# Four graph layers on one core: turned tiles read back from DRAM by one DMA, a new order of the work, dummy products on TensorE

## The chip, the cores and the metric

The kernel runs on one core of a Trainium2 chip. The metric is the device time of one execution in microseconds (us), the median of several runs. A core has TensorE (PE in the profile: matmuls; PEld: the loads of its weights), VectorE (DVE), ScalarE (ACT), GpSimd (POOL) and SyncE (SP). Here SP does nothing but issue DMAs, in order, on one queue.

## The reference, cut to what matters

64 graphs of 256 nodes with 256 features, and a 256 x 256 adjacency matrix each, go through four layers. Each one is `x = x + layer(relu(layernorm(x)), adj)`, all in float32:

```python
# layer 0: eight heads of 32
scores = where(adj > 0, q @ k.T / sqrt(32), -1e9);  x += (softmax(scores) @ v) @ Wo + bo
# layer 1: one head, softmax over axis 1
e = leaky(f1[:, None] + f2[None, :]);  x += elu(softmax(where(adj > 0, e, -9e15), axis=1) @ Wh)
# layer 2: three rounds of messages and a GRU cell
m = h @ weight[i];  aggr = A.T @ m;  h = gru(aggr, h)
# layer 3: four heads of 64
logits = leaky(s_src[:, None] + s_dst[None, :]);  out = softmax(where(adj == 1, logits, NEG)) @ f
```

Attention weights leave the softmax with a query in each partition, and the product that follows wants a key in each partition. So a 128 x 128 turn stands between them; one is needed too behind each norm and between the rounds of layer 2.

## The kernel before

**Tiles.** Two graphs make a pair, so there are 32 pairs. A pair's `x` is one tile of 128 partitions x 1024 (four chunks of 128 tokens). Most other tiles (`w4`, 21 slots) have this size too, 512 KB. The eight banks of PSUM (`ps`) hold 128 x 512 each.

**Tasks and order.** The functions `layer0` to `layer3` (L805, L940, L1054, L1225) do not issue instructions. They hand tasks to `Plan.add` (L195): an engine, a cost in us, a function that issues the instructions, and the buffers read and written. Some tasks have two forms, for instance an eviction on ACT or on DVE (`evict`, L414) or an addition on POOL or DVE (`either`, L421). `ORDER` (L48) is a compressed table, searched offline: it gives each of the 13,630 tasks a rank and a form. `Plan.order` (L240) walks the tasks by rank, gives each buffer the slot that comes free first by its estimated times, and returns the list in which every engine's instructions are issued. So each engine runs its own share of this list, in order, and waits where data is late. A DMA is taken to last its issue cost plus 1.4 times its `latency` (`SLOW`, L46 and L269). About six pairs are in flight at once.

**Turning through DRAM.** `through_dram` (L720) is used by `turn` (L732, attention weights), `turn_chunks` (L749, between rounds of layer 2) and `turn_rows` (L764, behind a norm). VectorE first turns blocks of 32 x 32 within the tile (STREAM_TRANSPOSE at L734, L755, L768). One DMA writes the 512 KB tile to a DRAM tile (L723). Four DMAs of 128 KB read it back (L726), each into 32 partitions, so that block column b of each block row lands in partitions 32b to 32b+31. The small turn at the end of layer 3 has the same shape (L1316, L1320, L1323). Tiles read back this way are `mixed`: their columns are in block order, and their readers use strided views (`wide`, `turned_keys`, `by_block`).

**Who turns how.** `TURNED` (L578) names the norms of layers 0 and 2 and the rounds of layer 2; they go through DRAM in all pairs but the last. The norm of layer 3 is turned by TensorE: eight 128 x 128 transposes against the identity (L664), then an eviction with relu on ACT (L676) or DVE (L677). The attention weights of layers 0 and 3 go through DRAM (those of layer 3 in the last pair by TensorE, L744).

**Products.** Most PE time goes to the gates of layer 2 (L1124, 128 x 512). The scores of layer 0 use 32-row tiles of the array (mode "rows", L844), its context product 32-column tiles ("columns", L896), layer 3's product 64-column tiles ("halves", L1300).

**Layer 3's end.** Per graph, eight `scalar_tensor_tensor` on DVE (L1334) scale the read-back tile by the reciprocal sums and add it to `x`. In layer 0, POOL adds the bias `bo` to `x` (L811).

Of the kernel before, what the change touches and what calls it, by code (L numbers as in the profile page):

```python
# [19 lines left out]
P = 128  # L20
# [17 lines left out]
class Task:  # L38
    __slots__ = ("pair", "forms", "form", "bufs", "rank", "stage", "mode", "before", "end", "engine", "latency")


class Plan:
# [3 lines left out]
    SLOW, SWITCH = 1.4, 0.19  # L46

    ORDER = (  # L48
        "c-rlI2Y_T%m3Ezb?|b*<S2=f8=iJki6U>kqh9FVNf`bxFxW-*vcSZDHRM1_+qO7>AxQa?rRz*hQNQMbaf?;y%?&;}R)m{1B{}wPamAa>TNTS"
        "m)-PKk1y?fvJ&iT%F&b^JSGxS-RKJ<7U64EsK?}%Y0r__{_Uj7&8U+e;ezYbn~=5t^|8eRr>NB1*mH>9AK9{<I<U8uk53z1K3{?Urxi6f5Qp"  # L50
        "L85YtP5wZZ@SSCI;`VY0Agr<EfaDCgryJGK(Ao(E2C;o?=fQTkzr5V#aIKFa#Nd>s5>pHWbHM_>$|64w^(2_*j$qy`J@LNQq%PQK<`58FlP~"
        "$<JEDo{#ESp7_z7CW5ce#tL#Wpf@eThz7NR=y5@}0kspJe)|$O2>umFYylNhQC@e^E0f2Te%2str2(qFGNjvbbF{ERFq&#gcA0UPGtUekhbK"
        "zCz59hn_{m1x->~fk2lAxkK5COxG4=@6cgSv;5{*V21VINSEKmd^d+9c365cS8qMSiO%HR#X)9F3MmcZz7~N&rF#&^iobfD~eh`*egbjDW`9"
        "1wS{JiI^V?IT=JRjmdV)g^7hzpaA%lfSSNr6;c5exo0VTkD-*FLK(XqA;2x$VwXE4A>5x~^YO*0(Ns-Z8EHf?cZ}|Ro=W?iIjO%@f|j(N{lF"
        "^(Ajq;fOlUfYEj(+LOfBDnTFVj;Q&WGwgD4zb1BRd<TA*t~%`kGt2w)}I5IoJfU%t^TWxRn?#&#&*@MA(e$GCUezY|mvYHL7g>}m7T`VRq?#"
        "a<*~S1$!06|SaI?rJwi9ylkKX#1j1Nx0A@quIKznsS=L2V;Z&PAbFBXrLcJR&!}8hnz5uH%%izMqC^snY$s33X}lK3a9*;8%pV-Ifm4%U)_x"
        "!v(Fa)2us26bgfXND^Q&Nztg2Q0e*rn0&ExS>iPJmXFqv@0JYL4h{#cZeLy;qL^qH+&|oLB3o4(bHBDH6%#>CNU<?50oe=H?IHP%m{&@H_nZ"
        "U!II>@i49iv=xMzdVQQZPr%aX5Pe47jt9<K967n%TJDNE!Q04f)RNPi=lS*54@PpFx3^R4Cro4H!p<EG+`(kG?#Y#x`{+E@56gMjq1B2~Um>"
        "bqF<vnA2P!fE}x;HW0G22i)-3=_a^+bB?is>pKB%xbhS3JwgIokd=nuCI}6&&Ax2&dP5A1tLC}#hTzXcZCs_7tZCo=q^JUd=C(oC*T6n%8ke"
        "l>02SQmwaBj8y?YmI-Oo-${sA|cZ=hX2c7ss^i;+lfk^n^dkter)^oGs=fUqDf<R~)X?u#Y<38>t42()L!R9}>PAmd&|I8F%S5_f)-5l?-Dh"  # L60
        "zNyzG?6ue0|v;yvR{sGjh+DCUMk!Vu48L<gtn@n+2LLn%tQQ^-F`@1V4n%!mTJ&GEW6w)9)wf84MWY}hpwOlKU&`+=Hsd!$aq9~?Z*EmxNbW"
        "}4d8}Lc|f{Gr(f(`bdn@K8TNoL!f_gv$7g0_)-?i@A(G?PgII8f7!&FR<g#Zn2q`h7=op{d_{({ZZ%ub)(S|M+XrrXs*PX2+9Evlc1!_qgt1"
        "N4^fN*JYqxHw^+)ZQF>`gNP!a^=|`JZ(Jp`?-XA*O{X6Ysf{hbzpiM=U3@lODV5W2FAmzpmdASmznV=R^DE+SjmuuP@c4r)22Zeeu5Ub@~~?"
        "?XF?#y4iM4Blxnrq?Kv|GjWuXTq78Zmjg1#<4AR+hE#BgxJxi!c^SkERc5(gN+v+gh{B?{!5+mTr`nlW&UUy3?)->Zt14E*2sas;m&@c{nGF"
        "OIA_N3M=XUHRVaW4dbf*-h*xMkE+XF)5tU4i}eGDFeD?NS}UA;6ie#sLj-;SckImx#jALdsG!5O1z9yhu^EZ8Bgc)0mtx@5dG?~&On35~Yk?"
        "F!gM9<z(aSaPM`VK=2S>;4@+<k2B8WcR3$)L*hIH6ZQ<hbVYKoW(5Gy3c3vEP*g;+SJn8W8Vv=nD;WMBR)=q(rCi2DG=^R2tOZ`u`d=U5e%K"
        "_nCY6W0BIaaqb~4dlR*}F%^L;U6q}a)y=IN@pi3we8Z0LG>?T01z{DVb=4*B~j9&c!20@v9u>~*AW6BewH@h|1cg}N;J@f9C{!AFkQgxiD*$"
        "^PR{VU%;^LM{i!4CSluby__bCSfAK=2afJ8N-=;DgpgYhb?P!|-k0%3ShCn6qoY7u*g^kBPLqujZsW4Njo_^!j$Bbi!%7S>jhZY6DmRbnq-~"
        "8T193rCIK@nMo)Rs<m>kW;PXIh(EpLnpcC!zt^2;7X|ysyls-;6rqmN;Zt`lLa$yhyY6!GlVfZ2u;Jb2cYai<7jBZzGeEi@iRTfpli52xo+p"
        "&{<^jcNALBWy4%O_G!Q<XC>)EK_sz>()XwU^B@<(>bj`qDy?qQ1_gz15(DN+ow5ex5daGpS0y<i{+qiMOUP@`I+W1JIRy|Le;$3qtBaSR4H5"  # L70
        "%`l4Z73(Z`rLLAo$P(4?lwK`=;QymOM632FArVCoiCDNauCgucT&#$Oc(7WOpFyTHLhB+t_wJ~Mx>benLqMGTNjfhALPho{a)*qFN;XT^JY2"
        "6G)_8S|M(aLT<gE{(KDZG=w10WX~tUS5HmIXCa&3iDqMTN$8&4gx6enX^)_w0&t=5AP~)`q{u|VjWq@P$Ipqd|^?<<XkT&JU2fE-C9((J)Is"
        "AcUfO-ha%f`MK@c?|G@r==~$37|%oxtM8z%xJew!o~FZk`3zXm1D`F7T$6)m;LRv;>^1DVGJq;PnFO2}Sq04DPsw2->2ayUu-L*>d!0_&$6_"
        "KQlUa%MuWzo~4(cDMl2$&W~XM5?~IkA6gfldEz<&RFO)i7=g{r;PCf_*MZ%s;WhGff$&UQM`66F$qGG)&VomvGw4C}gbM|n)z%9TBJgZ&hzk"
        "?Dy*`OEjXn!wjVHc(f#HUv+=C<`?hr9}Swz$lNfRec19{UOj++A`qBF?>7xDZ-(bL9_4FO7%HK=p%%pod?BW@5H<8|=AZQ~S4!_*|uW@U}Jd"
        "l7~1G|EL#LTR<UDR-Q5N`g}?;JoLvesYcTl?8EbXn>VVVumyz%1B_rT~0^btDL;=WB>bK4qx1^EnD`$$+hNUJGf{6=ubn_p>3XN`Xt%>#_=~"
        "ogO1&ajE?0&o|Hs6{NE3D-uY`UH&X4Vnjd#v6Lt)@`>wg?L_CvpTE=lT$Bnx^;)9@Ag2iPA8t{W8hvgJ`_E?a(eDm`JZRh63+`lmQtrMOR^@"
        "JB@NIUHx+VYfd`KQ;ymy|iahgJF5Q`Ver@~4L11Py3GyLnCyK$|j68PjrbZ2MD9E=YhM1s$MZUEsm6O|@$vY*8EYet_%5Om?oYmrrvh{U7@h"
        "Wa^a5K)>A6^o*f}05-_bpnwkD3F4^Z+H~3`36M~?ql1``6b#r!IF2qWLib~hrV|aIv<y*rk~<p8<`it`UX*Zbx|)mD5KdWL(2-Mi1S~UY1ff"
        "M6VXN>^otOp7!8Ik2+*h99YBHS6Xda}a?=lZt@(2ZD_jmNj4p&x)|M{Axe#0LgG6ZRtWEu&3`_}wrLLNBv>%aK<@-OFQyz`Em(sRB8$OX0Xb"  # L80
        "@O&!Ot~T5|Mb!)@BK#WqYyE&-7iK#^QMLcZOo0nbl>^#DV3(@cs}w6?X$<}M$8KxYLfhCTcEE?s#~%m^V!g6?1~B|A~H#GNa`F&X3x#wD^2P"
        "E>017*`b$a&f5bFxe+AhSP8!{L#ohmsyAykS+dS98ciYb9(Rz*?)i_&`pPdE@5_fX-(F{~vl3L?-pFJXbLW0tVgg`A%b|A<gkpb+-3VL3F#a"
        "yXCV_L~6up62T>EiDxXL*q-D-yU#PJc}yDu&%Sn3v_GBc{n7k<r?I?g%D|cSVK(k(ixp3e3fUgDE6q5y3%t5N4!}){dZL2?-~HIx7U3d0bjH"
        "i76I^W{~<C2BiH>3ho?qXI8F{XofUMgNp8jl(zB=lV`M;f=nqx&&N(h5JcSpFwMPN2r%ixFJNVTU;`KN{l|`?1Y)yRaV?6lKsh>aT+6IqJ_#"
        "O%(SxzMXKV&JX_)8CdU);QrXDw;Id|a;D=zvRp3dD2h$hqyr;s!2Mvb1n@Ew%6Q1F=eDT#lqb7rU~p!$;EQd?hb^LFlR%bZpJQ+d>sM2VMHy"
        "gUF;3ri`FawSd21njU>iM#!_0QYWTT#F8ZD2k{y*#}E}PtVys{Ts7?3QwU1v=~15=n|7719!B#3>O+k5ah{?G@=vT4>?cpG2}vVZg;ndN4)N"
        "&D_OIiKrO&u8uh4(5%MII6#o?~_-x-T-t&l^>lr_hw9&vCMevHAN8G%kk`**Pi?xP~!AlC6uc%>2Z`k7=P-E`6EFjsB%^VPH5mj=)Y3t?8qg"
        "Ko%#k7p>hp2`9&s_%;HSu_Ag2qwBa@co^e9oE9baEw&#cJ7*)rwKn(nm&);qtDIi(jsV2q?tBR!}xUj0AhafX=w;gYM?7O)(I}O}hX16`GLd"
        "`a}drpUSC08gKsO!uh7iFw9vB|MQqs!`;xUWwL$w7$e8Ow(L{g>M!gaLU@1Np+mE^&!A}y2d+!}{tujkkZ|RS<DcAPkX#6K+`4Y9%;h+l&xV"
        "aNr~d$gF*gE7!eC64ozaXXuQ-;IdXjPp)R0d|J0+ejxb`{!ehG=l=Z*z-o|9RA`uf&w@J09`T#svRMtf_tI{uiSJ;|V9=ohgR;WA{7BfHn-o"  # L90
        "bDrta$Yf@2G{gc+Qd0<A2&0G7fhJN!PNqm6Vmp?9iM1yhDYI2MHb|g8;`XPcwX`wZa~l5L%IY8Ze$K6Xklf>dhCcdio1dyo+dCQ7B`0O$@-O"
        ")n2}OS0Bdz=L;r1h%qfl9ld>Y#&sgo+a221bCIvziHSmm<Fb8$FM4H|Gp%?L}WvKgne1+}tG|jbvB5Q&UKCYC1DtevZkxU*cjp`_BB52u_$N"
        "L6bb_9ULBe{$2rCFTe=@PUgw-Jzs9@z2ih8oO}BL1oGGb^!~k>v=QvFtcX7=;DH%hb<D??ugAjc1smYJs&bJxgK5Eu&YSraA=-S8jC$ZZnOf"
# [189 lines left out]
def tile_adj_preln_d4(  # L283
# [100 lines left out]
    def buf(tag):  # L384
        return Buf(tag, tiles[tag])
# [1031 lines left out]
```

## Time and profile before

| what | before |
|---|---|
| median of 3 runs (lowest to highest) | 3498.58 us (3495.51 to 3502.81) |
| the profiled execution: its time, its span | 3501.53 us, 3499.7 us |
| mean granted TensorE clock | 0.993 |
| PE, DVE, ACT, POOL busy in 800 to 1600 us | 99.6%, 91.3%, 73.6%, 14.3% |
| DMA engines, mean busy share | 69.3% |
| DMAs: turn writes, read-backs | 535 and 2140 of the large, 62 and 248 of the small |

"Busy" of PE is the time covered by its records, each as long as its pipeline, so short gaps do not show in it; the distance from one start to the next does show them. A line such as "PE ps L664 <- DVE w L625: 5.8, 2, 3.5" says that TensorE's instructions of line 664, writing a `ps` tile, waited for VectorE's of line 625, writing a `w` tile: 5.8 us in 2 waits, the longest 3.5. In a timeline the columns are start, length, engine, line, operation, tiles, and how many instructions were merged.

### The profile page before, as it was taken

Reading aid. Unit: us, or ns where it says so; the run is one execution under the profiler, and the core shown is the slowest. Engines: PE = TensorE matmul, PEld = TensorE weight load, DVE = VectorE, ACT = ScalarE, POOL = GpSimd, SP = SyncE. Lnnn points to the kernel's source line nnn. Section 1 sums busy time; section 2 is a strip of 40 time slices with the busy share of each in tenths; the row PEclk is TensorE's granted clock in tenths of the full one; section 3 lists DMA queues with packets and bytes.
Section 4 is the critical chain, followed back from the end, with each engine's and each line's share of the span. In section 5 each row is a group of like instructions: output and inputs, shape, how many; then the busy total and the mean of one; then the engine's idle time right before and its main releaser. Section 6 shows DMA issues by size and latency. Waiting matters only on the chain.

```text
span 3499.7 us, 53732 instructions
## 1 busy us (share of the span) xinstructions
PE 3433.5 (98%) x14784; PEld 1931.6 (55%) x14784; DVE 3078.1 (88%) x9047; ACT 2522.0 (72%) x6739; POOL 453.1 (13%) x497
## 2 busy tenths in 40 slices
PE   8899999999999999999999999999999999999997
PEld 5555555555555555555555555555555555555554
DVE  8788998999999989999899888999889989889767
ACT  7756786766776777777767777778777768668545
POOL 1010110111111111111111111111011111011010
PEclk9999999999999999999999999999999999999998
DMA  8655877777677777777776777777677776576444
GB/s 287 209 150 167 248 240 217 224 229 228 212 217 233 226 222 235 223 225 225 218 230 215 228 227 216 235 230 234 214 228 216 234 224 218 183 220 201 155 131 136
DMA packets 596081, 753.41 MB, mean 215 GB/s; under 512 B 99012, under 2 KB 507076, under 8 KB 595780
## 3 DMA queue, kind: packets, MB, share of 16 engines
q1 hardware_dynamic: 595780, 749.98, 69.3%
q8 instruction: 118, 1.93, 0.2%
q14 instruction: 183, 1.50, 0.1%
HBM read 426.78 MB, written 314.59 MB: 212 GB/s over the span
## 4 chain that ended last, share of the span: by engine, by line
PE 64%; DVE 7%; DMA 3%; ACT 2%; issue 1%; SPq 1%; POOL 0%; DVEq 0%; ACTq 0%; POOLq 0%
PE ps L1124 37%; PE ps L823 4%; PE ps L1101 4%; PE ps L1246 3%; PE ps L844 3%; PE ps L1300 2%; PE ps L699 2%; PE ps L1031 2%; PE ps L896 2%; PE ps L1017 2%; PE ps L911 2%; DMA w<-turn 2%; DVE w L792 1%; DVE w L954 1%; DVE x L1334 1%
## 5 line engine op out<-in xcount | busy, mean ns | idle before, releaser
L1124 PE MATMUL ps<-w,whhT 128*128 128x512 f32 x2304 | 1071.2, 594 | 1.2 <-DVE mx L792 1.0
L1124 PE MATMUL ps<-w,giT 128*128 128x512 f32 x2304 | 1064.9, 593 | 0.0
L799 ACT ACTIVATE w<-w,mx 128x256 f32<-128x256 f32 x1536 | 759.2, 499 | 45.2 <-DVE mx L792 43.7
L1124 PEld LDWEIGHTS ps<-w,giT 128*128 128x128 f32 x2304 | 435.9, 190 | 534.5 <-issue 511.2
L1124 PEld LDWEIGHTS ps<-w,whhT 128*128 128x128 f32 x2304 | 430.4, 190 | 496.3 <-issue 451.4
L734 DVE STREAM_TRANSPOSE w<-w 128x1024 f32<-128x1024 f32 x380 | 466.4, 1234 | 45.2 <-ACT w L876 25.7
L417 ACT COPY w<-ps 128x512 f32<-128x512 f32 x431 | 244.2, 579 | 198.1 <-PE ps L1300 79.0
L792 DVE CUSTOM_DVE_ANT_0 w<-ps,mask 128x256 f32<-128x256 f32 x1024 | 370.8, 417 | 14.7 <-PE ps L844 12.6
L876 ACT ACTIVATE w<-w,rz 128x256 f32<-128x256 f32 x678 | 292.4, 498 | 88.4 <-DVE rz L869 85.1
L619 ACT ACTIVATE w<-x,rs 128x256 f32<-128x256 f32 x464 | 244.7, 591 | 93.3 <-DVE rs L611 88.9
L799 ACT ACTIVATION_READ_ACCUMULATOR w<-w,mx 128x1 f32 x1536 | 293.4, 191 | 0.0
L1181 POOL TENSOR_TENSOR w<-w,w 128x512 f32<-128x512 f32 x86 | 114.0, 1332 | 1147.9 <-PE ps L1124 368.4
L1277 ACT ACTIVATE w<-w,f 128x256 f32<-128x256 f32 x512 | 219.5, 499 | 16.1 <-DMA w<-row 10.0
L1101 PE MATMUL ps<-part,part 128*128 128x256 f32 x1536 | 228.8, 299 | 1.8 <-DVE part L1091 1.7
L605 POOL TENSOR_SCALAR rs<-mv 128x4 f32<-128x4 f32 x129 | 40.9, 317 | 1368.0 <-DVE mv L594 1301.1
L1149 ACT ACTIVATE w<-ps,brz 128x512 f32<-128x512 f32 x192 | 129.3, 677 | 123.1 <-PE ps L1124 113.4
L1101 PEld LDWEIGHTS ps<-part,part 128*128 128x128 f32 x1536 | 197.3, 190 | 32.1 <-issue 18.3
L792 DVE CUSTOM_DVE_ANT_0 w<-w,mask 128x256 f32<-128x256 f32 x512 | 196.4, 428 | 13.3 <-ACT w L1277 12.4
L1176 ACT ACTIVATE w<-w,bih_sb 128x512 f32<-128x512 f32 x192 | 136.5, 716 | 97.4 <-DVE w L1172 97.3
L592 DVE BATCH_NORM_STATS2 st<-x 128x6 f32<-128x256 f32 x512 | 189.1, 411 | 10.8 <-DMA x<-in_x_dram 8.2
L1163 ACT ACTIVATE w<-ps,brz 128x512 f32<-128x512 f32 x192 | 129.2, 677 | 75.5 <-PE ps L1124 73.1
L1154 DVE SCALAR_TENSOR_TENSOR w<-w,w 128x512 f32<-128x512 f32 x192 | 132.6, 692 | 44.4 <-ACT w L1149 28.1
(117 smaller groups left out, 5132.7 us busy)
## 6 DMA issues: line engine op xcount, KB each, us to landing
turn<-w SPq DMA_DIRECT2D x535, 512.0 KB
w<-turn SPq DMA_DIRECT2D x2140, 128.0 KB
w<-in_adj_dram SPq DMA_DIRECT2D x128, 512.0 KB
w<-row SPq DMA_DIRECT2D x64, 512.0 KB
x<-in_x_dram SPq DMA_DIRECT2D x64, 256.0 KB
out_dram<-x SPq DMA_DIRECT2D x64, 256.0 KB
turn<-w SPq DMA_DIRECT2D x62, 256.0 KB
w<-turn SPq DMA_DIRECT2D x248, 64.0 KB
```

The source lines that it names most:

```text
L417: (A, act(n), lambda: nc.scalar.copy(dst(), src())),
L592: nc.vector.bn_stats(st()[:, t, :], tok(xt())[:, t, :])
L619: nc.scalar.activation(tok(xn())[:, t, :], tok(xt())[:, t, :], func, bias=rs()[:, 1, t : t + 1], scale=rs()[:, 0, t : t + 1])
L734: add((V, dve(T * N), lambda: nc.vector.transpose(blocks(), blocks())), writes=[e])
L792: nc.vector.tensor_tensor_reduce(row, src, mask, scale, 3.0e38, ALU.add, ALU.min, mn)
L799: nc.scalar.activation(row(e, r), row(e, r), AF.Exp, bias=mn()[:, r : r + 1], scale=-1.0, accum_out=zs()[:, z0(r) : z0(r) + 1])
L823: mm(ps(), w[:, k, o * P : (o + 1) * P], wide(hT, k), start=k == 0, stop=k == 1)
L876: op(row, row, rz()[:, r : r + 1])
L1101: mm(ps()[:, o * N : (o + 1) * N], chunk_of(part(), h.mixed, c, o), tok(ams[g](), N)[:, c, :], start=i == 0 and c == 0, stop=i == 1 and c ...
L1124: mm(ps(), w[:, k, c0 : c0 + P], wide(src, k), start=n == 0, stop=n == 2 * len(terms) - 1)
L1176: (A, act(N2, 1), lambda o=o, hn=hn: nc.scalar.activation(at_o(hn, o), at_o(hn, o), AF.Tanh, bias=bih_sb[:, 4 + o : 5 + o])),
L1277: nc.scalar.activation(dst, src, AF.Prelu, bias=f()[:, t, D + h : D + h + 1], alpha=ALPHA)
```

## The change

1. **One read-back.** The four reads become one DMA over all 128 partitions: partition p = 4j + b takes block column b of row j. So that the result comes out in the order wanted, VectorE's block transposes read their source with a distance of four elements between neighbours (L768, L755 and L1316), and so do the mask (L784), the keys in TensorE's scores product (L847) and ScalarE's first step in layer 3 (L1276).
2. **Layer 3's norm** goes through DRAM as well, in all pairs but the last.
3. **Layer 3's product** is cut into 32-column tiles; its end is two multiplications by the reciprocals and one addition, on POOL or DVE. Adding `bo` may go to DVE too.
4. **The plan** models DMAs anew: per DMA an issue time, a time `dma` on one shared lane, a `latency` and 1.2 us of `LANDING`, with eight in flight at most, in place of 1.4 times a latency. The order is searched anew (11,870 tasks). Many costs are refitted.
5. **Dummy products.** Where the plan expects PE to idle for over 1 us (after its first 20 us) and a PSUM bank is free, it inserts 128 x 128 transposes of the identity worth half of that idle time.

```diff
-    TURNED = ("0", "2", "2m",)
+    TURNED = ("0", "2", "3", "2m")
...
+            if engine == "SP":
+                begin = max(begin, lanes[0])
+            if engine == "PE":
+                idle = begin - free.get("PE", 0.0)
+                spare = [slot for at, slot in slots["ps"] if at <= free.get("PE", 0.0)]
+                if idle > self.IDLE and spare and begin > 20.0:
+                    out.append(lambda n=int(self.FILL * idle / 0.11), slot=spare[0]: self.busy(slot, n))
+                    now = "full"
...
-            t.end, t.engine = begin + us + t.latency * self.SLOW, engine
+            if engine == "SP":
+                free["DMA"] = max(free["SP"], free.get("DMA", 0.0)) + t.dma
+                t.end, t.engine = free["DMA"] + t.latency + self.LANDING, engine
+                lanes = lanes[1:] + [t.end + 0.1]
...
+    def busy(slot, n):
+        for i in range(n):
+            nc.tensor.transpose(tiles["ps"][slot][:, 0:P], ident, ident)
...
     def through_dram(e, eT):
         d = buf("turn")
-        add((SP, 0.6, lambda: nc.sync.dma_start(d(), e())), reads=[e], writes=[d], latency=4.6)
-        for b in range(4):
-            add(
-                (SP, 0.55, lambda b=b: nc.sync.dma_start(
-                    eT()[32 * b : 32 * b + 32, :].rearrange("p (a w) -> p a w", a=4),
-                    d()[:, b * N : (b + 1) * N].rearrange("(a j) w -> j a w", a=4))),
-                reads=[d], writes=[(eT, b)], latency=3.8,
-            )
+        add((SP, 0.41, lambda: nc.sync.dma_start(d(), e())), reads=[e], writes=[d], latency=1.41, dma=1.36)
+        add(
+            (SP, 0.5, lambda: nc.sync.dma_start(
+                eT().rearrange("p (a w) -> p a w", a=4),
+                bass.AP(tensor=d().tensor, offset=d().offset, ap=[[N, P], [32 * T * N, 4], [1, N]]))),
+            reads=[d], writes=[eT], latency=2.04, dma=1.9,
+        )
...
-                e().rearrange("p (b x i) -> p x b i", b=4, i=32), xn().rearrange("p (x b j) -> p x b j", b=4, j=32))),
+                e().rearrange("p (b x i) -> p b x i", b=4, i=32), xn().rearrange("p (x j b) -> p b x j", b=4, j=32))),
...
-                                tok(kT(), N2)[r, cc, g * N : (g + 1) * N].rearrange("p (c b j) -> p b c j", c=2, b=4),
+                                else tok(kT(), N2)[r, cc, g * N : (g + 1) * N].rearrange("p (c j b) -> p b c j", c=2, b=4),
...
+                            for r in range(0, C3, 32):
+                                mm(
+                                    pso()[j * C3 + r : j * C3 + r + 32, k * N : (k + 1) * N],
+                                    f()[:, 2 * g + c, h * C3 + r : h * C3 + r + 32],
...
+                def divided(o=o, rz=rz):
+                    for j in range(2):
+                        oj = o().rearrange("p (j a y i) -> p j a y i", j=2, a=2, i=32)[:, j]
+                        rj = rz().rearrange("p (y j) -> p j y", j=2)[:, j]
+                        nc.vector.tensor_tensor(oj, oj, rj.unsqueeze(1).unsqueeze(3).to_broadcast([P, 2, 4, 32]), ALU.mult)
...
+                add(either(0.0, to_x), reads=[o], writes=[(xt, g)])
```

The table's bytes can be read without running anything: the last third of them is each task's form. Counted over pairs 3 to 28, per pair: VectorE takes 2.0 of the 4 scalings behind the norms of layers 0 and 3 (0.58 before), 2.5 of the 6 casts L1085/L1086 (0.62), 1.04 of the 2 new additions to `x`, 0.5 of the 2 additions of `bo` (none); the shares of the other tasks shift by less. Changes between full products and tiled ones number 10.5 a pair (10.0 before).

## The prediction

> **What bounds the kernel.** I read the page's first lines, then the chain, the timeline of one pair, TensorE's waits, and the group rows of what the change touches.
>
> ```profile
> span 3499.7 us, 53732 instructions
> PE 3433.5 (98%) x14784; PEld 1931.6 (55%) x14784; DVE 3078.1 (88%) x9047; ACT 2522.0 (72%) x6739; POOL 453.1 (13%) x497
> ...
> PE 64%; DVE 7%; DMA 3%; ACT 2%; issue 1%; SPq 1%; POOL 0%; DVEq 0%; ACTq 0%; POOLq 0%
> ```
>
> PE is busy 98% of the span and carries the chain. VectorE follows at 88%; in the middle (800 to 1600 us) it stands at 730.5 of 800 us, 91%. In the chain, the same step comes back once a pair:
>
> ```profile
> 2365.94 7.06 PE ps L823 x16
> ...
> 2470.89 7.06 PE ps L823 x16
> ```
>
> That is 104.95 us a pair. In a timeline of PE around there, instructions follow without a gap, the transposes of layer 3's norm among them:
>
> ```profile
> 2438.63 1.88 PE L1124 MATMUL ps<-w,giT 128*128 128x512 f32 x4
> 2440.35 1.04 PE L664 MATMUL ps<-ident,w 128*128 128x128 f32 x8
> 2441.22 1.88 PE L1124 MATMUL ps<-w,whhT 128*128 128x512 f32 x4
> ```
>
> From start to start the eight transposes take 0.87 us, 109 ns each. So I counted PE's time by starts: each kind of instruction at its usual distance to the next (429 ns for 512 columns, 216 for 256, 109 for a transpose, a quarter of 216 on a 32-wide tile) makes 3328 us. A change between full and tiled products adds 93 ns (523 in place of 429); 10.0 of them a pair are 30 us. The first product starts at 6.9 us, the last ends 4.8 before the end. What remains, 3499.7 - 3328 - 30 - 11.7 = 130 us, is waiting and slow clock: about 39 in the first 200 us, 63 in the middle, 28 after 3440. TensorE's waits on read-backs (the columns are us in total, times, longest), and two rows of the chain that show a turn's DMAs when they are waited for:
>
> ```profile
> PE ps L896 <- DMA w<-turn: 12.8, 4, 8.4
> ...
> PE ps L1300 <- DMA w<-turn: 2.0, 1, 2.0
> ```
>
> ```profile
> 2981.34 5.66 DMA w<-turn
> ...
> 3185.46 6.47 DMA turn<-w
> ```
>
> **Layer 3's norm leaves TensorE.** 31 pairs lose eight transposes: 31 x 0.87 = 27.0 us. PE runs without gaps there, so this stands on the path; what is late next is the next product, ready already. In exchange a pair gets one more STREAM_TRANSPOSE, one more 512 KB write and read, and a relu from SBUF in place of one from PSUM. The new wait is relu on DMA: behind it stand the four products of L1246 and, on ACT or DVE, whatever the order put there. A pair is in flight for some 620 us and six overlap, so some ten microseconds more latency is covered by other pairs' products; without that cover it costs a pair 5.66 + 6.47 = 12 us once, at the end, where pair 30 may show it.
>
> **Mode changes.** 10.5 rather than 10.0 a pair: 0.44 x 0.093 x 32 = +1.3 us. Cutting layer 3's product into 32 columns is free by the rows: two products take 3.59 us at L896 (32 columns) and 3.60 at L1300 (64).
>
> **VectorE.** The rows of what it gains and loses:
>
> ```profile
> L768 DVE STREAM_TRANSPOSE w<-w 128x1024 f32<-128x1024 f32 x62 | 76.7, 1238 | 17.3 <-ACT w L619 11.6 <-PE ps L1124 5.2
> ...
> L1334 DVE SCALAR_TENSOR_TENSOR x<-w,rz,x 128x64 f32<-128x64 f32 x496 | 111.9, 296 | 0.2
> ```
>
> Per pair: transpose +1.24; scalings +1.42 x 2 x 0.457 (L625) = +1.30; casts +1.88 x 0.415 (L1086) = +0.78; additions to x 1.04 x 0.69 (L1218) = +0.72; four multiplications of 128 x 256, by L1221's and L876's rows about 0.37 each, +1.5; sixteen of L1334 at 111.9/496 = 0.226, -3.6; other forms cancel. Sum +1.9 us. Today 0.913 x 104.95 = 95.8, then 97.8 of a pair's 104.1 us: 94%. It stays below PE, and costs nothing while it does.
>
> **Distance-four reads.** No row has them. Touched per pair: three transposes of L768 (3.7 us), three of L755's pairs (3.9), two of L1316 (1.4), four halves of the mask L782 (1.8), in all 10.8 us of VectorE; on PE four score products (4.3 us). From below 0: L734 in place, L768 and L755 with scattered runs all take 1.2 to 1.3 ns an element, so the order of reading has bought nothing so far. From above I take a doubling: 10.8 us of DVE and 4 x 0.85 of PE a pair. The nearest row is L755, whose blocks already lie scattered over the tile in runs of 32: 688 ns for 512 elements, as L1316's 705. I take 0 and keep the other end as a rival. "SBUF — State Buffer" in the Trainium skill, section on Door 1, says SBUF is read in lines of 16 bytes, that float32 may be strided by up to four for free, and that an access which crosses to a new line pays. Four floats are 16 bytes, a new line with each element; by the first half the sum stays, by the second it goes towards the doubling; no run here shows it yet.
>
> **One read for four.** SP issues 2140 + 248 read-backs in about 0.48 us each; 628 remain, 1760 x 0.48 = 845 us of SP's time go, and the last quarter is issued three issues (1.4 us) earlier. SP's in-order queue stands behind each write's wait as before, once instead of four times. The bytes per transfer stay: the 16 engines were busy 69%; one more turn a pair adds 128 packets of 4 KB (177 ns) and 512 of 1 KB (58 ns) over 16 engines, 3.3 us of 104, and fewer completions take back half a per cent: some 72%. Nothing of it is on PE's path by itself; it can only shorten waits, of which PE's on `turn` reads are 14.8 us. Bounds: 0 to -15; it goes into the next term.
>
> **The new order.** It can win no more than the 130 us of waits and slow clock. The start is bound by DMA (97% busy in 20 to 40 us), the tail by the last pair's chain, whose forms stay. The order written for one model is not shown by any row to be better on the chip. Bounds: half of the 130 gone (-65), or a wait of 2.1 us in each pair (+65, below). I take -17, about a quarter of the middle's 63, since waits on `turn` are the largest kind there.
>
> **Dummies.** They fill half of the waits that the plan expects. Where a wait is real they cost nothing and keep the clock: behind the waits of the tail, eight instructions of L1246 take 3.89 us where sixteen take 3.72 in the middle; counting such rows the slow clock costs 6 to 7 us there and 4 to 5 in the first 200 us. Where there is no wait they delay: at worst half of today's 66 us of visible PE idle, +33. I take -5.
>
> **Sum**, against the profiled execution: 3501.5 - 27.0 + 1.3 - 17 - 5 = 3453.8. It was 2.95 above the median: **3451 us**.
>
> **Rivals.**
> *Waits eat part.* PE's saving stands, but the new order's waits are no shorter, or up to 19 us longer: 3473 to 3492. For it: PE already waits little in the middle. Chance 0.17; the next 14 us, no change, 0.06.
> *The order cuts turns too fine: slower.* The old model gives a write 0.6 + 1.4 x 4.6 = 7.0 us and the reads 0.55 x 4 + 1.4 x 3.8 = 7.5; the new one 4.4 and 5.6 on an empty lane, 4.5 less per turn, 18 turns a pair. The chain shows 6.47 for a write. If one product a pair (L896 or L1300) comes 6.47 - 4.4 = 2.1 us too early, 31 x 2.1 = +65, so 3451 + 22 + 65 = 3538; from 26/31 = 0.83 us a pair on it is slower than before. Against it: the new model adds what other DMAs hold the lane. Chance 0.10.
> *VectorE becomes the bound.* Distance-four reads double: 97.8 + 10.8 = 108.6 us a pair, PE waits, +3.65 x 31 = +113, so 3612; from 66% on it is slower. Chance 0.05.
> *The change moves products instead of saving them*: 27 us of dummies (248, from 54 us of expected waits) where nothing waits: 3473. It lies in the first rival.
>
> **How the numbers follow.** Forecast 0.62 (3410 to 3473), the others 0.17, 0.06, 0.10, 0.05. A measurement here tells some 0.2% (7 us) from no change: faster 0.62 + 0.17 = 0.79, same 0.06, slower 0.15. Range 3418 to 3494: the slower cases and a sliver of either end are left out, under 0.2.
>
> **What would show it.** L664 falls from 272 to 24 instructions, PE's period to about 104; STREAM_TRANSPOSE rows keep 1238 and 688 ns, L782's rows 491; score groups keep 1.08 us; reads count 566 and 62. Wrong, if PE waits on `w<-turn` or on DVE grow beyond some 25 us, if DVE's share passes 96%, or if dummies stand where the next product was ready.

## The result, and the profile after

The changed kernel takes **3679.61 us** (median of 4 runs, 3677.77 to 3681.47), against 3497.62 us before, measured beside it (median of 4, 3495.51 to 3502.81): a ratio of 1.0518, 95% interval 1.0500 to 1.0536. It is 182 us slower, where 47 us faster was forecast. The profiled execution took 3678.88 us, its span is 3676.8.

The page of the changed kernel, the lines that answer to those shown of before:

```profile
span 3676.8 us, 52134 instructions
PE 3561.3 (97%) x15659; PEld 1916.8 (52%) x15659; DVE 3311.9 (90%) x8901; ACT 2569.2 (70%) x6584; POOL 468.3 (13%) x512
...
q1 hardware_dynamic: 587956, 782.38, 63.7%
```

TensorE is busy for 128 us more although it has less to do: 27 us of transposes are gone, and 99 dummies of 109 ns from start to start (10.8 us) have come. VectorE is busy 234 us more, ScalarE 47. The DMA engines have become less busy (69.3% before). So the transfers do not look like the source of the time; instructions that each got longer do.

The groups of the changed kernel that read with a distance of four (total busy time, mean ns of one), and the in-place transpose, which does not:

```profile
L805 DVE STREAM_TRANSPOSE w<-w 128x1024 f32<-128x1024 f32 x93 | 190.8, 2053 | 16.1 <-ACT w L657 15.0
L792 DVE STREAM_TRANSPOSE w<-w 128x512 f32<-128x512 f32 x186 | 195.8, 1092 | 2.5
L1365 DVE STREAM_TRANSPOSE w<-w 128x512 f32<-128x512 f32 x62 | 69.1, 1114 | 3.4 <-ACT w L450 2.2 <-ACT w L923 0.5
L819 DVE TENSOR_SCALAR mask<-w 128x512 bf16<-128x512 int32 x126 | 77.1, 657 | 0.7 <-DMA w<-in_adj_dram 0.7
L1325 ACT ACTIVATE w<-w,f 128x256 f32<-128x256 f32 x512 | 353.6, 749 | 40.4 <-DMA w<-row 22.7 <-DVE w L1220 9.3 <-DVE w L1229 3.3
L891 PE MATMUL ps<-w,w 32*128 32x256 f32 x2048 | 265.5, 639 | 19.3 <-ACT w L450 10.8 <-DVE w L451 7.4 <-ACT w L1197 0.9
...
L771 DVE STREAM_TRANSPOSE w<-w 128x1024 f32<-128x1024 f32 x380 | 464.8, 1232 | 20.1 <-ACT w L836 9.4 <-ACT w L923 8.2
```

Before, the first six stood at 1238, 688, 705, 491, 499 and 399 ns. Rows of before:

```profile
L755 DVE STREAM_TRANSPOSE w<-w 128x512 f32<-128x512 f32 x186 | 120.9, 688 | 2.6
L782 DVE TENSOR_SCALAR mask<-w 128x512 bf16<-128x512 int32 x126 | 56.6, 491 | 0.3 <-DMA w<-in_adj_dram 0.2
L1277 ACT ACTIVATE w<-w,f 128x256 f32<-128x256 f32 x512 | 219.5, 499 | 16.1 <-DMA w<-row 10.0 <-PE ps L896 2.3 <-DVE w L734 2.1
L844 PE MATMUL ps<-w,w 32*128 32x256 f32 x2048 | 149.5, 399 | 4.7 <-ACT w L417 2.9 <-DVE w L418 0.9 <-DVE mx L792 0.7
```

Every reader at distance four is 34 to 66% longer; the transpose that reads its neighbours (L771, formerly L734) is as it was. TensorE's own part is plain in its timeline, where a group of sixteen score products (L891, formerly L844) stands between products of the gates, first before, then after:

```profile
2489.68 1.15 PE L844 MATMUL ps<-w,w 32*128 32x256 f32 x16
2490.76 1.98 PE L1124 MATMUL ps<-w,whhT 128*128 128x512 f32 x4
```

```profile
2042.87 2.06 PE L891 MATMUL ps<-w,w 32*128 32x256 f32 x16 [1.52 <-DVE w L451]
2044.86 1.98 PE L1172 MATMUL ps<-w,whhT 128*128 128x512 f32 x4
```

From the start of the group to the next product it is 1.99 us, where it was 1.08. In 128 groups that is 116 us of TensorE's path with nothing late at all. The wait ahead of the group (1.52 us) is a second kind of loss. TensorE's longest waits of the changed kernel (total us, times, longest) are now on VectorE and ScalarE, and those on read-backs have all but gone (14.8 us before). Its waits on VectorE add up to 73.4 us, where they were 23.4:

```profile
PE ps L1149 <- DVE part L1139: 13.1, 20, 2.5
PE ps L891 <- ACT w L450: 10.8, 13, 2.4
...
PE ps L1349 <- DMA w<-turn: 1.4, 1, 1.4
```

To see where the time is lost I put TensorE's starts into a ledger, as in the prediction: the usual distance of each kind of instruction makes the stream; what a start comes later than that is lost. The last column is a kernel of the experiments below: the changed kernel, but with no distance in its reads.

| us | before | after | after, all reads in runs of 32 |
|---|---|---|---|
| span | 3499.7 | 3676.8 | 3453.0 |
| stream by usual distances | 3328.0 | 3311.7 | 3311.7 |
| ahead of the first start | 6.9 | 4.9 | 4.8 |
| lost in the first 200 us | 40.2 | 37.7 | 29.7 |
| lost from 200 to 3400 us | 90.8 | 291.1 | 87.4 |
| lost after 3400 us | 28.9 | 26.6 | 14.5 |
| behind the last product's end | 4.8 | 4.7 | 4.7 |

After and the last column have the same instructions, the same order and the same transfers. Of the 224 us between their spans, 204 are lost in the middle, spread over all of it. A part of this loss is slower clock: the granted clock of TensorE is 0.989 over the span of the changed kernel and 0.997 over that of the last column, so (1 - 0.989) x 3676.8 = 40 us of full clock are missing in the one and 10 in the other. By this estimate up to 30 of the 224 us are clock; the ledger does not separate them from the waits.

### The profile page after: what moved, and what is told of

Same layout as the page of the kernel before. It is cut to its first block, busy times and chain, and to the rows that moved or that the text cites. A ratio compares the mean times of both kernels' runs of the same rounds, so it can differ in the third digit from the quotient of the medians.

```text
span 3676.8 us, 52134 instructions
## 1 busy us (share of the span) xinstructions
PE 3561.3 (97%) x15659; PEld 1916.8 (52%) x15659; DVE 3311.9 (90%) x8901; ACT 2569.2 (70%) x6584; POOL 468.3 (13%) x512
## 5 line engine op out<-in xcount | busy, mean ns | idle before, releaser
L1172 PE MATMUL ps<-w,whhT 128*128 128x512 f32 x2304 | 1085.9, 599 | 13.3 <-DVE w L1240 6.8
L771 DVE STREAM_TRANSPOSE w<-w 128x1024 f32<-128x1024 f32 x380 | 464.8, 1232 | 20.1 <-ACT w L836 9.4
L1325 ACT ACTIVATE w<-w,f 128x256 f32<-128x256 f32 x512 | 353.6, 749 | 40.4 <-DMA w<-row 22.7
L450 ACT COPY w<-ps 128x512 f32<-128x512 f32 x443 | 247.9, 579 | 174.1 <-PE ps L1149 51.4
L657 ACT ACTIVATE w<-x,rs 128x256 f32<-128x256 f32 x390 | 207.5, 592 | 134.0 <-DVE rs L649 121.8
L891 PE MATMUL ps<-w,w 32*128 32x256 f32 x2048 | 265.5, 639 | 19.3 <-ACT w L450 10.8
L1229 POOL TENSOR_TENSOR w<-w,w 128x512 f32<-128x512 f32 x96 | 127.4, 1331 | 1207.8 <-ACT w L1224 1087.7
L1149 PE MATMUL ps<-part,part 128*128 128x256 f32 x1536 | 261.5, 315 | 19.5 <-DVE part L1139 13.1
L1149 PEld LDWEIGHTS ps<-part,part 128*128 128x128 f32 x1536 | 205.2, 192 | 93.3 <-issue 43.7
L805 DVE STREAM_TRANSPOSE w<-w 128x1024 f32<-128x1024 f32 x93 | 190.8, 2053 | 16.1 <-ACT w L657 15.0
L1197 ACT ACTIVATE w<-ps,brz 128x512 f32<-128x512 f32 x192 | 129.2, 677 | 99.0 <-PE ps L1172 88.1
```

Source lines behind the costliest of these rows:

```text
L450: (A, act(n), lambda: nc.scalar.copy(dst(), src())),
L657: nc.scalar.activation(tok(xn())[:, t, :], tok(xt())[:, t, :], func, bias=rs()[:, 1, t : t + 1], scale=rs()[:, 0, t : t + 1])
L771: add((V, dve(T * N), lambda: nc.vector.transpose(blocks(), blocks())), writes=[e])
L805: (V, dve(T * D), lambda: nc.vector.transpose(e().rearrange("p (b x i) -> p b x i", b=4, i=32), xn().rearrange("p (x j b) -> p b x j", b=4 ...
L891: mm(banks[hh]()[:, cc * N : (cc + 1) * N], tok(qT(), N2)[r, cc, t * P : (t + 1) * P], tok(kT(), N2)[r, cc, g * N : (g + 1) * N] if early ...
L1149: mm(ps()[:, o * N : (o + 1) * N], chunk_of(part(), h.mixed, c, o), tok(ams[g](), N)[:, c, :], start=i == 0 and c == 0, stop=i == 1 and c ...
```

## The experiments

Two theories were to be told apart. **The reads:** the distance of four makes VectorE, TensorE and ScalarE slow. **The order:** the plan behind the new order, or its one large transfer, brings the waits. Under the second, little more than the 116 us of the score products would come back without the distance. Each ratio below is against the kernel before, run beside it (medians 3498.5 to 3503.1); "+" figures are against 3448.79 us, the median of the second kernel below (runs_of_32_one_read), and carry the 4 us or so by which those medians of before differ.

**1. All reads in runs of 32, four DMAs again (four_reads).** The new order, norm and dummies stay; the output is the reference's.

```diff
-  xn().rearrange("p (x j b) -> p b x j", b=4, j=32)
+  xn().rearrange("p (x b j) -> p x b j", b=4, j=32)
# alike in L793, L821, L895, L1324, L1366
-  eT() <- ap=[[N, P], [32 * T * N, 4], [1, N]]
+  eT()[32 * b : 32 * b + 32] <- d()[:, b * N : (b + 1) * N]    for b in range(4)
```

> The changed kernel with the old read-back: four DMAs per turn, issued one behind the other by the same task, and with it all reads of VectorE, ScalarE and TensorE in runs of 32 again. Order, layer 3's norm through DRAM, plan and dummies stay. Theory 1 (distance-four reads): the score products give back 116 us (TensorE's busy time at that line went from 149.5 to 265.5 us) and VectorE some 190 us (STREAM_TRANSPOSE 2053 for 1238 ns and 1092 for 688, masks 657 for 491), so TensorE is the bound again: 3440 to 3490 us, STREAM_TRANSPOSE at 1238 and 688 ns. Theory 2 (the new order itself waits more): only the 116 us of the score products return: 3540 to 3570 us.

Measured: 3466.98 us (3460.08 to 3471.37), ratio 0.9906 [0.9891, 0.9921]. It is faster than both kernels; none with the reference's output was faster in these runs. The new order is no cause of the loss.

**2. Runs of 32, one DMA (runs_of_32_one_read).** As the first, but with the changed kernel's DMA.

> The changed kernel with one DMA per read-back as it is, but all reads of VectorE, ScalarE and TensorE in runs of 32. Keys, tokens and features reach the later products in a shuffled order, so the output is not the reference's; the amount of work is the same. Beside four_reads it shows what one DMA in place of four is worth. Theory 1: within 15 us of four_reads, and below it if TensorE's waits on turned tiles matter: 3430 to 3490 us. Theory 2: 3540 to 3570 us.

Measured: 3448.79 us (3448.28 to 3455.07), ratio 0.9860 [0.9845, 0.9875]. This is the forecast, 3451, within 3 us, in a kernel that does the same work on shuffled keys, tokens and features. Page and groups of this kernel:

```profile
span 3453.0 us, 52134 instructions
...
PE 3404.0 (99%) x15659; PEld 1896.5 (55%) x15659; DVE 3108.2 (90%) x8901; ACT 2448.7 (71%) x6584; POOL 466.5 (14%) x512
```

```profile
L805 DVE STREAM_TRANSPOSE w<-w 128x1024 f32<-128x1024 f32 x93 | 115.3, 1240 | 20.2 <-ACT w L657 19.0
L891 PE MATMUL ps<-w,w 32*128 32x256 f32 x2048 | 141.6, 397 | 5.8 <-ACT w L450 5.1 <-DVE mx L829 0.8
L1325 ACT ACTIVATE w<-w,f 128x256 f32<-128x256 f32 x512 | 227.1, 499 | 37.8 <-DMA w<-row 26.3 <-DVE w L1220 7.8 <-PE ps L943 2.0
```

The same instructions, the same count, the old durations. VectorE's share of the span is 90% here and 90% in the changed kernel: the share does not show the loss, because the span grew with the busy time. The mean duration of one instruction shows it.

**3 and 4. Half of the distances (scores_runs_of_32, vector_runs_of_32).** From the changed kernel, one DMA. In the first only TensorE's keys are read in runs; in the second only VectorE's transposes and masks are.

```diff
# scores_runs_of_32
-  kT ... rearrange("p (c j b) -> p b c j", c=2, b=4)
+  kT ... rearrange("p (c b j) -> p b c j", c=2, b=4)
# vector_runs_of_32: the same in L793, L806, L821, L1366
```

> The changed kernel, only the keys of TensorE's score products read in runs of 32 (the mask then meets the wrong keys; the work is the same). Theory 1: TensorE gets 116 us back, but VectorE, still with distance-four reads, needs 103.5 us of a pair's 104, so TensorE waits for it more than before: 3570 to 3620 us, not the full 116 below 3680. Theory 2: the full 116: 3560 to 3565 us.

> The changed kernel, only VectorE's transposes and masks read in runs of 32, TensorE's score products and ScalarE's first step of layer 3 still at distance four (shuffled keys; the work is the same). Theory 1: VectorE's load falls from 103.5 to some 97.5 us a pair, TensorE's stays at 107.7, and the waits beyond it shrink: 3580 to 3610 us. Theory 2: VectorE was not what TensorE waited for: 3660 to 3680 us.

Measured: 3615.32 us (1.0333 [1.0316, 1.0350]) with TensorE's reads mended, 3584.28 (1.0244 [1.0228, 1.0259]) with VectorE's mended. Neither alone brings the time back: 64 and 95 us of 231.

**5 and 6. The distances in the kernel before (before_scores_distance_4, before_vector_distance_4).** Only the patterns are changed, with the old order and the old four DMAs.

```diff
# before_scores_distance_4, L847
-  "p (c b j) -> p b c j"
+  "p (c j b) -> p b c j"
# before_vector_distance_4: the same in L755, L768, L784, L1316
```

> The kernel before, only the keys of TensorE's score products read at a distance of four elements (they then meet the wrong masks; the work is the same). If distance-four reads cost TensorE by themselves, whatever the order: the group of sixteen goes from 1.08 to about 2.0 us, four a pair, 32 pairs: +116 us, 3610 to 3625 us. If the cost came from the new order: 3500 us.

> The kernel before, only VectorE's block transposes (two norms, three rounds of layer 2, two small ones a pair) and masks read at a distance of four (shuffled keys and features; the work is the same). VectorE gets 5.5 us more a pair: 101 of 105 us. If VectorE costs something only above TensorE's own time: 3500 to 3510 us. If a nearly full VectorE makes TensorE wait before it is full, as the 3615 us of scores_runs_of_32 suggest: +50 to +110 us, 3550 to 3610.

Measured: 3600.68 us (1.0290 [1.0275, 1.0305]), a little below the expected range, and 3578.24 us (1.0227 [1.0211, 1.0242]), within it. TensorE's group of the first (399 ns before), then VectorE's of the second:

```profile
L844 PE MATMUL ps<-w,w 32*128 32x256 f32 x2048 | 266.2, 641 | 1.7 <-ACT w L417 0.8 <-DVE w L418 0.6 <-ACT w L1277 0.2
```

```profile
L755 DVE STREAM_TRANSPOSE w<-w 128x512 f32<-128x512 f32 x186 | 197.2, 1102 | 2.6
...
L768 DVE STREAM_TRANSPOSE w<-w 128x1024 f32<-128x1024 f32 x62 | 129.0, 2082 | 16.1 <-ACT w L619 10.8 <-PE ps L1124 5.0
```

An access pattern and nothing else makes a kernel whose order is fixed for the old durations 2 to 3% slower. With that the theory of the order has fallen as a cause of the slowdown: the patterns do the same harm without it.

**7 to 10. One kind of read at a time (scores_only, transposes_only, scalar_only, masks_only).** Each is the second kernel with a single kind put back to distance four.

```diff
# on runs_of_32_one_read, one of these in each
scores_only_distance_4       L895              "p (c b j) -> p b c j"       ->  "p (c j b) -> p b c j"
transposes_only_distance_4   L793, L806, L1366 "p (x b j) -> p x b j"       ->  "p (x j b) -> p b x j"
scalar_only_distance_4       L1324             "p (c h b j) -> p h c b j"   ->  "p (c h j b) -> p h c b j"
masks_only_distance_4        L821              "p (t c b j) -> p c t b j"   ->  "p (t c j b) -> p c t b j"
```

> runs_of_32_one_read (3449 us) with TensorE's score products alone at a distance of four (keys meet the wrong masks; the work is the same). If TensorE's cost stands by itself on the path: +100 to +116 us as in the old order, 3549 to 3565. If the waits beside it swallow part: under 3540.

> runs_of_32_one_read with VectorE's block transposes alone at a distance of four (shuffled tokens and features). They add 5.6 us a pair to VectorE's 97. If a pace near VectorE's own time is what counts: 97 + 5.6 = 102.6 of TensorE's 103.6 us, with waits +90 to +140, 3540 to 3590 us. If VectorE is covered while it stays below TensorE: 3449 to 3460.

> runs_of_32_one_read with ScalarE's first step of layer 3 alone at a distance of four (749 in place of 499 ns, sixteen a pair: 4 us of ScalarE a pair, which is busy 71% of the time; the keys meet the wrong masks). If only a full engine costs time: 3445 to 3455 us. If the order leaves no room on the way from these steps to layer 3's product, as the 50 us of attention_one_read over four_reads suggest: 3470 to 3500.

> runs_of_32_one_read with the masks' reads alone at a distance of four (VectorE, 657 in place of 441 ns, four a pair, 0.9 us; masked keys are shuffled). The pieces so far add 101 (scores), 108 (transposes) and 48 us (ScalarE) to 3449; all together 231. If the pieces' costs overlap and the mask's is small, as layer0_one_read suggests: +5 to +25, 3454 to 3474. If the mask holds up every score: +30 or more.

| distance four in | median us | ratio to before | + us | longer busy time, us |
|---|---|---|---|---|
| scores (TensorE) | 3550.20 | 1.0146 [1.0129, 1.0163] | 101 | PE 117 |
| transposes (VectorE) | 3556.98 | 1.0162 [1.0147, 1.0177] | 108 | DVE 177 |
| first step of layer 3 (ScalarE) | 3496.46 | 0.9983 [0.9974, 0.9993] | 48 | ACT 128 |
| masks (VectorE) | 3461.26 | 0.9886 [0.9872, 0.9901] | 12 | DVE 26 |

The four make 269 us; together they cost 231, so their costs overlap a little. TensorE pays 0.87 of each us that it is busy longer, VectorE's transposes 0.61, and ScalarE 0.37, though ScalarE is busy only 73% of the span. The scores in scores_only_distance_4, and two of the transposes in transposes_only_distance_4, which are 1240 and 687 ns in the second kernel:

```profile
L891 PE MATMUL ps<-w,w 32*128 32x256 f32 x2048 | 258.2, 637 | 3.6 <-ACT w L450 3.6
```

```profile
L792 DVE STREAM_TRANSPOSE w<-w 128x512 f32<-128x512 f32 x186 | 196.2, 1095 | 2.5
...
L805 DVE STREAM_TRANSPOSE w<-w 128x1024 f32<-128x1024 f32 x93 | 191.3, 2057 | 15.9 <-ACT w L657 14.7
```

Each kind has its long duration by itself, whatever the others do. One way on which ScalarE's time reaches the path shows in VectorE's waits on its first step, first without and then with the distance:

```profile
DVE w L829 <- ACT w L1325: 5.5, 11, 1.3
```

```profile
DVE w L829 <- ACT w L1325: 36.3, 64, 1.6
```

VectorE, itself busy 89 to 90%, stands 31 us longer at the masked minimum that follows ScalarE's step, and its later work for TensorE comes later: in TensorE's waits, those on L1139 go from 3.9 to 7.5 us and those on ScalarE's evictions (L450) from 5.1 to 12.5. All of TensorE's waits on these two engines together go from 35.4 to 60.9 us. That is about half of the 48 us; where the rest arises was not followed.

**11 and 12. Other distances (distance_2, distance_8).** The second kernel, with TensorE's keys and the norms' transposes read at another distance (one run each).

```diff
# distance_2
-  kT ... "p (c b j) -> p b c j"         xn() ... "p (x b j) -> p x b j"
+  kT ... "p (x j u) -> p x u j", u=2    xn() ... "p (b x j y) -> p b x y j", y=2
# distance_8
+  kT ... "p (j u v) -> p u v j", u=4, v=2    xn() ... "p (b j y) -> p b y j"
```

> runs_of_32_one_read with TensorE's score products and the block transposes behind the norms read at a distance of two elements, 8 bytes (the products meet shuffled keys). If the cost grows with the number of 16-byte lines touched: half of the loss, group of sixteen 1.3 to 1.5 us, transposes 1.4 to 1.65 us. If only a distance of four or more costs: 1.08 and 1.24 us. If any distance costs the same: 2.0 and 2.05 us.

> The same two reads at a distance of eight elements, 32 bytes. If each element of a new 16-byte line costs a fixed time: as at four, 2.0 us a group and 2.05 us a transpose. If the distance itself counts: up to 3.8 and 3.7 us.

Measured: 3452.14 and 3578.70 us. The groups at distance two, then at eight:

```profile
L891 PE MATMUL ps<-w,w 32*128 32x256 f32 x2048 | 147.4, 404 | 5.2 <-ACT w L450 4.5 <-DVE mx L829 0.6
...
L805 DVE STREAM_TRANSPOSE w<-w 128x1024 f32<-128x1024 f32 x93 | 115.5, 1242 | 19.5 <-ACT w L657 18.3
```

```profile
L891 PE MATMUL ps<-w,w 32*128 32x256 f32 x2048 | 262.7, 646 | 4.6 <-ACT w L450 4.6
...
L805 DVE STREAM_TRANSPOSE w<-w 128x1024 f32<-128x1024 f32 x93 | 189.9, 2043 | 17.7 <-ACT w L657 16.6
```

Two costs nothing, four and eight cost the same. The step lies between two and four float32.

**13. One DMA in the old order (before_one_read).** The kernel before with its tasks and rank; the first of the four read tasks issues the whole read, the others nothing.

> The kernel before, its old order and all its reads, with one DMA per read-back, issued where the first of the four stood (shuffled keys and features; the work is the same). If the 18 us between four_reads and runs_of_32_one_read come from the read-back itself (SP's issues, a later last quarter): 3475 to 3490 us. If they come from the new plan, which counts one issue per read and is late with four: 3495 to 3503.

Measured: 3492.64 us (10 runs), ratio 0.9976 [0.9966, 0.9986]: 6 us, between the two ranges. In the new order the same exchange is worth 18 us (3466.98 to 3448.79). The transfers themselves are lighter. The queue's row (packets, MB, share of the 16 engines) in four_reads, then in runs_of_32_one_read:

```profile
q1 hardware_dynamic: 618100, 782.50, 73.4%
```

```profile
q1 hardware_dynamic: 587956, 782.38, 67.1%
```

The 30,000 packets that are gone carry almost nothing (4 bytes each, by their sizes in the trace), the bytes are the same, and a packet of 1 KB takes 49.9 ns on average in place of 57.9.

**14. Without dummies (four_reads_no_dummies).** The first kernel, with the plan's insertion of dummies left out.

> four_reads without the 99 dummy transposes. If they keep the clock in the waits of start and tail as the prediction took it (5 us, at most 11): 3470 to 3478 us beside four_reads' 3467. If they do nothing or delay: 3460 to 3468.

Measured: 3470.06 us (3468.18 to 3474.81), ratio 0.9914 [0.9898, 0.9931], 3 us above four_reads. The two intervals overlap; the dummies do no harm, and a gain of a few us is not shown. That they keep the clock is: over the last 100 us of the profiled span, where 94 of the 99 stand, the granted clock is 0.97 in four_reads and 0.88 without them. The kernel before and its three variants have 0.87 to 0.89 there, the kernels with dummies 0.93 to 0.99. The dummies themselves take 10 us of TensorE's time there.

**15 and 16. One DMA with the reference's output, for the attention turns (attention_one_read, layer0_one_read).** The in-place transposes of the attention weights need no distance if the keys already come in the other order. For layer 0, K is put into that order as it leaves PSUM; layer 3's first step on ScalarE and the masks read at distance four; all other turns keep four DMAs. The second of the two does it for layer 0 alone, so only layer 0's mask has the distance.

```diff
-  evict(tok(dst(), N2)[:, o, :], ps)
+  evict(tok(dst(), N2)[:, o, :].rearrange("p (x b j) -> p x b j", b=4, j=32),
+        ps().rearrange("p (x j b) -> p x b j", b=4, j=32))        # for K
```

> Four reads for norms, rounds and small turns, in runs of 32, but one read for the twelve attention turns a pair; the distance-four reads that these need fall on the eviction of the keys from PSUM (two a pair, ScalarE or VectorE), on ScalarE's first step of layer 3, and on the masks (VectorE, 0.66 us a pair); TensorE's score products read runs of 32. If one read is worth 18 us for eighteen turns as between four_reads and runs_of_32_one_read, and ScalarE has the room: 3450 to 3462 us. If the added work on the way of the keys and masks costs as much as the reads save: 3463 to 3475.

> four_reads with one read for the eight attention turns of layer 0 alone; the keys are brought into the other order where they are evicted from PSUM (its group's mean stayed at 579 ns in attention_one_read), the mask of layer 0 is read at a distance of four (VectorE, 0.33 us a pair), ScalarE's step in layer 3 stays in runs of 32. If ScalarE's step made attention_one_read slow and one read is worth about 1 us per turn kind of the eighteen: 3455 to 3465 us, below four_reads. If the mask (on the way of every score) or the eviction made it slow: 3475 to 3500.

Measured: 3517.43 us (1.0052 [1.0037, 1.0067]) and 3467.86 us (0.9907 [0.9892, 0.9922]). Both missed what I hoped for. I had left ScalarE's step out of the price; with what the single kinds measured later, 48 us for that step, 12 for the masks and 12/18 of 18 us saved by 12 of 18 large read-backs, the first should stand near 3467 + 48 + 12 - 12 = 3515. For layer 0 alone, half of the masks (+6) against 8/18 of 18 us (-8) leaves nothing that can be measured, as found.

**17. The distance on the writing side (scattered_writes).** As attention_one_read, but every step reads its source in order and writes apart: the masks, ScalarE's first step, and the norms of layers 0 and 3 (which then come back by one DMA too).

```diff
-  mb  "p (t b c j) -> p c t b j"  <-  at  "p (t c j b) -> p c t b j"
+  mb  "p (t b c j) -> p c t j b"  <-  at  "p (t c j b) -> p c t j b"
# alike: row(e, r) "p b (c j) -> p c j b";  xn "p (x b j) -> p x j b"
```

> The reference's output, with every distance moved from the reading side of a step to its writing side: the masks and ScalarE's first step in layer 3 read their source in its own order and write neighbours far apart (128 bytes apart in the mask, 4 KB apart in layer 3's tile), the norms of layers 0 and 3 write their columns apart in the same way (128 bytes), the keys of layer 0 are put apart where they leave PSUM. VectorE's transposes, TensorE's scores and ScalarE's first step then read without a distance, and 14 of the 18 large turns of a pair are read back by one DMA (the norm and the rounds of layer 2 keep four). If the price is one of reading SBUF alone, L1331's ACTIVATE falls from 750 to 499 ns, the masks from 650 to 441, L657's stay at 592, and the time is that of one DMA in most places: 3449 to 3460 us. If writing apart costs as reading does, L1331 stays at 750, L657 rises from 592 towards 850 as well, and the time is at or above attention_one_read's 3517, to some 3560.

Measured: 3554.70 us, ratio 1.0150 [1.0134, 1.0167]. Writing apart costs as well. Two groups of this kernel:

```profile
L1333 ACT ACTIVATE w<-w,f 128x256 f32<-128x256 f32 x512 | 309.0, 719 | 42.3 <-DMA w<-row 26.0 <-DVE w L1210 8.6 <-DVE w L798 4.8
...
L825 DVE TENSOR_SCALAR mask<-w 128x512 bf16<-128x512 int32 x126 | 165.5, 1525 | 0.8 <-DMA w<-in_adj_dram 0.8
```

ScalarE's step stays near that, at 719 ns on the group's mean (750 read apart), the mask goes from 650 (read apart) to 1525 (bf16 written apart), and of the norm's scalings the ones written apart take 815 ns on ScalarE and 547 on VectorE in place of 590 and 439 (by the pattern of each instruction in the trace). So the price of the distance does not go away when it is moved to the writing side of SBUF, and for the mask it is higher there.

## Why the prediction was wrong, point by point

**The step that failed** is "Distance-four reads": "I take 0 and keep the other end as a rival." The patterns cost 231 us, and a kernel without them runs at the forecast. Three things went wrong in it.

- *The nearest row was not near.* I took L755, "whose blocks already lie scattered over the tile in runs of 32", for a row that speaks on distance. A run of 32 is distance one for 31 of 32 reads. No row of before had any distance, and the bounds, 0 to a doubling, should both have been given weight. I gave 5% to a mechanism that I could not exclude.
- *The list of what is touched was short.* It named VectorE's steps and the scores, but not ScalarE's first step in layer 3 (L1277 of before), which the change lists. It is 128 us of ScalarE, 4.1 a pair, and 48 us of time by itself.
- *The rival's price was for VectorE alone.* "VectorE becomes the bound" was set at 3612, with 10.8 us a pair on VectorE. Through the distances VectorE's instructions grew by 204 us, 6.5 a pair, not 10.8 (the transposes became 58 to 66% longer; the masks 34% against the 491 ns of before, 49% against the 441 of the second kernel). The scores, for which I had noted 4 x 0.85 us a pair as the upper end, took 4 x 0.91, and for these VectorE did not have to become the bound: TensorE was the bound already, so they count at once.

The page I cited has both halves of the answer. The Trainium skill, "SBUF — State Buffer", in its specifications asks for at least two accesses in a 16-byte line for full bandwidth; the runs agree: two float32 apart (two in a line) is free, four and eight (one in a line) cost alike. The free stride of four float32 that its section on Door 1 gives is not what these runs show: 1242 ns at two, 2053 at four.

**"It stays below PE, and costs nothing while it does"** was wrong as a rule. ScalarE at 73% cost 0.37 us per us, VectorE at about 92% 0.61 in the transposes. My reading is that the engines run lists that were fixed for other durations: a longer step makes its own reader late, and that one the next, long before the engine is full. The waits in scalar_only_distance_4 fit that, but no run searched the order anew for the longer durations, so whether a new order would hide part of the cost is open. The sign that I named, a VectorE share above 96%, never came: it stood at 90% in the changed kernel.

**What was right, and what only in sum**, read from the second kernel (same order, no distance):

- *Layer 3's norm leaves TensorE*, -27.0: L702 has 24 transposes left of 272, the stream is 27.0 us shorter before the dummies' 10.8. Layer 3's first products (L1294, formerly L1246) wait for the turned norm in the last pair alone, which still turns on TensorE (1.4 us, on L714).
- *VectorE*, +1.9 us a pair: +0.97 (30.1 us in 31 pairs). The forecast was twice what came, without consequence.
- *One read for four*, 0 to -15: -6 in the old order, -18 in the new, a little beyond the end. The DMA share fell to 67.1%, where I had 72%.
- *The new order*, -17, "about a quarter of the middle's 63": the size of the sum was right, the split and the place were not. By the medians four_reads is 33.4 us below the kernel before, of which the norm is 27.0; so order, mode changes and dummies together won some 6 us, and the single read, which I had put into this term, won 18. Together that is 24, where the terms (+1.3 - 17 - 5) made 20.7. By the ledger the middle gave only 3.4 us: in four_reads it loses 95.2, 4.4 more than before, and the single read brings that to 87.4. The start, which I had excluded ("the start is bound by DMA"), gave 10.5 + 2.1. The tail, excluded too ("the tail by the last pair's chain, whose forms stay"), lost 14.4 us less, but the 94 dummies that stand there take 10.2 of them in the stream.
- *Dummies*, -5: they keep the clock as forecast (0.97 for 0.88 in the last 100 us); what they gain in time is not told apart from 0 to -6.
- *Sum*: 3451 against 3448.79. That terms of it were off in both directions is hidden in this agreement, and that it is within 3 us is luck in part.

**The rivals.** "The order cuts turns too fine" and "waits eat part" did not happen: TensorE's waits on read-backs fell from 14.8 to 1.4 us, 1.5 without the distances. Of "VectorE becomes the bound" the premise came in part, as the reads got longer by a third to two thirds, but VectorE did not become the bound. The scores and ScalarE's step, which this rival left out, cost 101 and 48 us by themselves.

**The signs.** Pattern-free rows (L771), reads (566 and 62) and L702's count were as named; STREAM_TRANSPOSE at 2053 and 1092 ns, the mask at 657 and the score groups at 1.99 us refuted the step directly. One sign of being wrong came as named: TensorE's waits on VectorE grew by 50 us, from 23.4 to 73.4 (22.0 without the distances). TensorE's pair, taken as the mean over eight kinds of product from the seventh to the twenty-seventh pair, went from 105.8 to 112.8 us; without the distances it is 105.3, not 104. Most of that gap is the base: I had read 104.95 from one pair, where the mean was 105.8, so the norm's 0.87 us alone leads to 104.9; the rest is the gain that came in the start and not in the middle.

What stays open: why one read is worth three times as much in the new order as in the old one; whether a version with the reference's output can keep the 18 us; whether an order searched for the longer durations would hide part of the loss. By its layout, a read-back by two DMAs of 64 partitions each should need a distance of two only, which cost nothing in distance_2; that was not tried.

## What to carry to other kernels

Before a permutation is moved from the DMAs into the engines' access patterns, find the row that has the same innermost distance, not one whose blocks are scattered; if there is none, give both bounds weight, and price the upper one on every engine that reads the tile, TensorE's moving operand and ScalarE too. In this kernel an engine with a tenth or a quarter of its time free was no cover for longer instructions, with the order of work left as it was. When a change with several parts loses, undo the parts one at a time: here the order, the norm and the transfer were worth 49 us, and six access patterns cost 231 us.

## What the runs showed of the hardware

- Reading float32 four apart in SBUF: VectorE's STREAM_TRANSPOSE of 1024 elements 1240 to 2053 ns, of 512 687 to 1092; a mask from int32 441 to 657 ns (512 elements); ScalarE's activation of 256 elements 499 to 749 ns; sixteen products with 256 moving columns on 32-row tiles 1.0 to 2.0 us. Two apart, the transpose of 1024 and the products showed no difference (1242 and 404 ns). Eight apart, they were as at four (2043 and 646 ns).
- Writing apart costs too: float32 32 elements apart 590 to 815 ns on ScalarE and 439 to 547 on VectorE (256 elements); bf16 64 apart, from an int32 source, 441 to 1525 ns (512 elements).
- Reading PSUM four apart and writing SBUF in runs cost nothing: in attention_one_read 48 evictions of K on ScalarE took 581 ns on average, the 395 plain ones 579; on VectorE 679 and 680 ns.
- One DMA over 128 partitions in place of four over 32, at the same bytes and packets of the same size: 1 KB packets 49.9 ns in place of 57.9.
- Dummy transposes in TensorE's waits keep the granted clock: 0.93 to 0.99 in the last 100 us of the kernels that have them, 0.87 to 0.89 in the five that do not. A gain in time beyond the spread of the runs is not shown (3470.06 us without, 3466.98 with).
